# A row transform and an inverse product in the TensorE: the table becomes the stationary operand, the results are turned through device memory

## The chip, the cores and the metric

The kernel runs on one core of a Trainium2 chip. The metric is the device time of one launch, in microseconds (us); lower is better. Engines are called as the profile calls them: PE (matmuls) and PEld (PE's loads of its stationary operand), DVE, ACT, POOL, and SP, which here only issues DMAs.

## What is computed

64 images of 96 channels and 56 x 56 pixels go through three blocks. The reference, cut to what matters:

```python
# block 1: expand 96->192 (1x1) + silu, shift, 3x3 depthwise + identity + silu, gate, project 192->96, + x, silu
# block 2, per image, h of 192 channels over 3136 pixels in a row:
h = relu(bn(einsum('bnc,hc->bnh', layernorm(x), w1)))
X = jnp.fft.fft(h, axis=1, norm='ortho')          # along the 3136 pixels
xr = relu(X.real * rd - X.imag * idg + rb)        # and xi likewise
# ... inverse transform of the real result, product with w2 (192->96), bn, + x
# block 3: layernorm, 96->384->96 with 8-bit and 16-bit rounding, + x
```

The transform of length 3136 = 56 x 56 is done in two steps, each of them a product with a table of cosines and sines: first along one of the two factors ("rows", step f1), then along the other (step f2). Because the input is real, only 29 of the 56 frequencies of the first step are kept (NK = 29). On the way back, after the product with w2, step i1 multiplies by the table of the second factor and step i2 by that of the first.

## The kernel before

**Order of the work.** Every image is cut into named steps (ea_mm, dw_mm, ..., o_st), each a small function that issues one group of instructions; a name's ending tells the engine: `_mm` PE, `_ev` an evacuation by ACT (or DVE for w1_ev and i2_ev), `_ld`, `_st`, `_in` a DMA issued by SP. The table PLAN (L43) holds a time for every instance of every step and PERIOD (L42) the distance between images. The loop at L944 to L951 sorts all instances of all 64 images by `b * PERIOD + when` and issues them in that order. The times set nothing but this order: each engine works through its own instructions in it and waits by semaphores for what they need. So in the middle of the run PE works on parts of three or four images by turns, and an instruction that waits holds up all that PE has behind it.

**The steps around the change**, for one image:

- w1_mm (L642): 8 groups of matmuls, in each of them up to 8 columns of 56 pixels for both halves of the channels (hc), into one of two shared PSUM buffers of 2 banks (`mix_ps`, L378; w1, f1, f2, w2, i1 and i2 take them by turns). w1_ev (L658, DVE) applies relu and the scale and writes `buf_h`, channel by channel, 56 pixels each; partitions 0 to 55 hold channels 0 to 95, partitions 64 to 119 channels 96 to 191.
- f1_mm (L671): for each of 96 channel pairs the image's 56 columns are the stationary operand and the table `f_tab` streams (58 columns), twice, into both halves of PSUM's partitions: 192 products in 6 groups. f1_ev (L685, ACT): 12 copies into `buf_g`.
- f2_mm (L696): product with `l_tab`; f2_u, f2_s, f2_r, f2_p (ACT and DVE): the frequency filter, into `buf_h` (pq_a, pq_b). w2_mm (L762) and w2_ev (L790): product with w2, back into `buf_g` (u_v).
- i1_mm (L802): for each of 96 output channels a 112 x 32 block of `u_v` is the stationary operand and `inv_tab` streams (56 columns), for r = 0 and 1: 192 products in 3 groups of 64. i1_ev (L818, ACT): 3 copies into `buf_h` (p_v).
- i2_mm (L823): 112 products in 4 groups; a 64 x 48 block of p_v is stationary, 56 columns of `r_tab` stream; two of them lie in opposite quarters of the array. i2_ev (L840, DVE): 8 additions onto the image `t`.
- Then n_*, x_* (layer norm and turning), h_*, o_* (block 3), o_st (output by SP).

A product of 32-bit operands takes two passes, each a weight load (LDWEIGHTS) and a matmul of its own in the profile, so all these counts double there: 384 pairs per image at L676 (f1), 384 at L809 (i1), 224 at L831 (i2).

**DMAs.** In the loop SP issues, per image, 14 loads of x (L192), 14 stores of the output (L932) and 2 small transfers (L635). In the setup POOL issues ten loads between memsets (L216 to L347), ACT some others.

## Time and profile before

| what | value |
|---|---|
| median of 3 runs | 7425.91 us (7415.92 to 7431.19) |
| profiled execution: span from first to last instruction | 7414.7 us, 11.2 us under the median |
| PE / PEld / DVE / ACT / POOL busy | 7188.3 / 5229.7 / 4842.3 / 4641.4 / 1589.9 us |
| PE instructions | 177666 matmuls and as many weight loads |
| granted TensorE clock, mean | 0.993 |
| DMA | 185.34 MB, mean 25 GB/s |

The profile's page lists busy time by engine, the span in 40 slices, the DMA queues, the chain of work that ended last, and the costliest groups of instructions by line; "issue" means that an engine stood still and waited for nothing that the profile shows. The times in the text that go beyond the page come from the groups by line and shape, the order in time, and the waits of the same trace.

### The profile page before, as it was taken

Reading aid. Unit: us, or ns where it says so; the run is one execution under the profiler, and the core shown is the slowest. Engines: PE = TensorE matmul, PEld = TensorE weight load, DVE = VectorE, ACT = ScalarE, POOL = GpSimd, SP = SyncE. Lnnn points to the kernel's source line nnn. Section 1 sums busy time; section 2 is a strip of 40 time slices with the busy share of each in tenths; the row PEclk is TensorE's granted clock in tenths of the full one; section 3 lists DMA queues with packets and bytes.
Section 4 is the critical chain, followed back from the end, with each engine's and each line's share of the span. In section 5 each row is a group of like instructions: output and inputs, shape, how many; then the busy total and the mean of one; then the engine's idle time right before and its main releaser. Section 6 shows DMA issues by size and latency. Waiting matters only on the chain.

```text
span 7414.7 us, 383547 instructions
## 1 busy us (share of the span) xinstructions
PE 7188.3 (97%) x177666; PEld 5229.7 (71%) x177666; DVE 4842.3 (65%) x8790; ACT 4641.4 (63%) x9806; POOL 1589.9 (21%) x1366
## 2 busy tenths in 40 slices
PE   7999999999999999999999999999999999999997
PEld 5777777777777777777777777777777777777775
DVE  5666667666666666666666666666666666666674
ACT  3566666566665666666656666566666666666665
POOL 1221222212212122122121221221212212212222
PEclk9999999999999999999999999999999999999998
DMA  2010110110101101011011011110110111101100
GB/s 52 18 28 20 28 27 19 28 24 23 28 20 28 26 20 28 21 27 28 18 29 26 20 28 23 25 27 19 30 26 20 28 23 24 28 20 28 27 20 21
DMA packets 424334, 185.34 MB, mean 25 GB/s; under 512 B 378786, under 2 KB 422042, under 8 KB 422474
## 3 DMA queue, kind: packets, MB, share of 16 engines
q1 hardware_dynamic: 420794, 159.01, 9.3%
q8 instruction: 1392, 22.81, 1.3%
q0 software_dynamic: 528, 1.50, 0.1%
q14 instruction: 212, 1.73, 0.1%
q10 hardware_dynamic: 1408, 0.28, 0.0%
HBM read 82.80 MB, written 77.07 MB: 22 GB/s over the span
## 4 chain that ended last, share of the span: by engine, by line
PE 93%; ACT 3%; issue 3%; DVE 1%; POOL 0%; DMA 0%; POOLq 0%; ACTq 0%; SPq 0%
PE ps_d L469 14%; PE psa L676 9%; PE psa L649 9%; PE ps_ea L406 5%; PE ps_eb L423 5%; PE psa L831 5%; PE ps_n L580 5%; PE ps_pj L555 5%; PE psa L768 5%; PE psa L809 4%; PE ps_c L580 4%; PE psa L703 4%; PE ps_h L888 4%; PE ps_o L910 3%; PE psa L713 3%
## 5 line engine op out<-in xcount | busy, mean ns | idle before, releaser
L926 POOL TENSOR_TENSOR o<-t,o 112x448 f32<-112x448 f32 x448 | 659.1, 1471 | 3629.9 <-DVE o L920 2280.0
L469 PE MATMUL ps_d<-e_a,diag 32*32 32x392 f32 x36864 | 1029.5, 498 | 0.7 <-ACT d L479 0.7
L898 DVE TENSOR_SCALAR y<-y,qb 128x448 f16<-128x448 f16 x1344 | 483.1, 384 | 761.5 <-ACT y L893 748.4
L491 DVE SCALAR_TENSOR_TENSOR d_last<-e_b,taps,d_last 128x1568 f32<-128x1568 f32 x512 | 972.5, 1899 | 9.3
L469 PEld LDWEIGHTS ps_d<-e_a,diag 32*32 32x32 f32 x36864 | 659.8, 103 | 299.6 <-issue 37.5
L591 DVE TENSOR_REDUCE v<-sq 112x4 f32<-112x384 f32 x896 | 490.6, 548 | 480.7 <-ACT sq L587 479.7
L893 ACT CAST y<-ps_h 128x448 f16<-128x448 f32 x1344 | 682.6, 543 | 165.7 <-PE ps_h L888 157.8
L860 POOL TENSOR_TENSOR rs<-v,mhalf 112x4 f32<-112x4 f32 x448 | 489.5, 1097 | 1264.2 <-DVE v L592 1264.2
L649 PEld LDWEIGHTS psa<-w1c,t 112*64 112x64 f32 x14336 | 609.0, 137 | 178.0 <-issue 86.4
L904 ACT CAST h<-y 128x448 fp8e5<-128x448 f16 x1344 | 733.0, 570 | 2.2 <-DVE y L898 2.0
L676 PEld LDWEIGHTS psa<-f_tab,buf_h 128*56 128x56 f32 x24576 | 650.4, 131 | 111.0 <-ACT buf_g L688 45.4
L649 PE MATMUL psa<-w1c,t 112*64 112x96 f32 x14336 | 688.4, 249 | 3.4 <-DVE buf_h L661 1.8
L676 PE MATMUL psa<-f_tab,buf_h 128*56 128x58 f32 x24576 | 675.6, 216 | 1.1 <-DVE buf_h L661 1.1
L609 POOL TENSOR_TENSOR rs<-v,mhalf 112x4 f32<-112x4 f32 x448 | 461.1, 1034 | 917.2 <-DVE v L592 763.3
L566 DVE TENSOR_TENSOR ps_pj<-ps_pj,x 112x392 f32<-112x392 f32 x512 | 260.6, 566 | 546.0 <-issue 326.1
L572 ACT ACTIVATE t<-ps_pj,pjbn_b 112x392 f32<-112x392 f32 x512 | 289.6, 621 | 413.5 <-DVE ps_pj L566 413.5
L661 DVE SCALAR_TENSOR_TENSOR buf_h<-psa,rs_full 128x768 f32<-128x768 f32 (+1 forms) x512 | 430.8, 852 | 148.7 <-PE psa L649 148.7
L688 ACT COPY buf_g<-psa 128x464 f32<-128x464 f32 x768 | 388.8, 551 | 186.4 <-PE psa L676 184.7
L411 ACT ACTIVATE e_a<-ps_ea 128x448 f32<-128x448 f32 x448 | 237.6, 551 | 427.3 <-PE ps_ea L406 427.2
L809 PE MATMUL psa<-inv_tab,buf_g 112*32 112x56 f32 x24576 | 373.3, 214 | 99.3 <-issue 97.5
L809 PEld LDWEIGHTS psa<-inv_tab,buf_g 112*32 112x32 f32 x24576 | 327.5, 110 | 197.5 <-issue 196.3
L866 DVE TENSOR_TENSOR xt<-ps_n,rs 112x384 fp8e5<-112x384 f32 x448 | 243.7, 556 | 315.8 <-POOL rs L860 311.4
(176 smaller groups left out, 12984.4 us busy)
## 6 DMA issues: line engine op xcount, KB each, us to landing
x<-in_x SPq DMA_DIRECT2D x896, 84.0 KB, 2.7
out_dram<-o SPq DMA_DIRECT2D x896, 84.0 KB, 2.1
l_tab<-in_tab_l SPq DMA_DIRECT2D x1, 1624.0 KB, 6.9
r_tab<-in_tab_r SPq DMA_DIRECT2D x1, 1568.0 KB
t<-dev_t SPq DMA_DIRECT2D x64, 7.0 KB, 1.8
t<-dev_t SPq DMA_DIRECT2D x64, 5.2 KB
ex_row_p<-in_expand_row POOLq DMA_DIRECT2D x1, 336.0 KB, 4.3
s_p<-in_bn POOLq DMA_DIRECT2D x1, 288.0 KB, 4.6
```

What stands on the lines that cost most here:

```text
L469: nc.tensor.matmul(pss[r][j * 32 : j * 32 + 32], lhsT=diag[pr, tap, :], rhs=e_a[pr, r0 : r0 + PJ, dx : dx + HW], start=tap == 0, stop=tap ...
L491: nc.vector.scalar_tensor_tensor(d_last, win, w, d_last, ALU.mult, ALU.add)
L580: nc.tensor.matmul(cen[c0:c1, k, 0:C], lhsT=t_of(b)[:, n0 + c0 : n0 + c1], rhs=center, start=True, stop=True)
L591: nc.vector.tensor_reduce(v, sq, AX.X, ALU.add)
L649: nc.tensor.matmul(ps[hc * 64 : hc * 64 + 64, k, 0:C], lhsT=t[:, n0 : n0 + 64], rhs=w1c[:, hc * C : hc * C + C], start=True, stop=True,)
L676: nc.tensor.matmul(ps[r * 64 : r * 64 + HW, k, 0 : 2 * NK], lhsT=buf_h[:, n0 : n0 + HW], rhs=f_tab[:, r, :], start=True, stop=True,)
L809: nc.tensor.matmul(ps[p0 : p0 + 32, k, 0:HW], lhsT=u_v[:, oh * 48 + o, :], rhs=inv_tab[:, r, :], start=True, stop=True,)
L860: nc.gpsimd.tensor_tensor(rs, held.pop(("nv", b, g)), mhalf[0:CP, 0:4], ALU.pow)
L893: nc.scalar.copy(y16, held.pop(("h", b, i)))
L898: nc.vector.tensor_scalar(y16, y16, qb1[:, i % 3 : i % 3 + 1], 0.0, ALU.add, ALU.max)
L904: nc.scalar.copy(held["h8", b, j][:, m, :], held.pop(("y", b, i)), saturate=False)
L926: nc.gpsimd.tensor_tensor(o32, rows, o16, ALU.add)
```

## The change

Four things are done together.

- **f1.** The table is the stationary operand (`f_tab`, now 56 rows by 64 columns, for both halves of the partitions), and the image streams: 4 columns of pixels by 96 channels, 384 columns in one product. There are 7 groups of 4 products, one for each half of the channels (hc, the upper or lower half of the array's rows) and each parity of the pixel column (d, the left or right half of its columns). So w1_ev now writes `buf_h` pixel by pixel. The result has the frequency on the partitions, where f2 wants the pixel column there; f1_ev (7 copies) puts it into a work tile `fs`, f1_st (new, SP) stores it to device memory (`spec`), and f2_ld (new, SP, 12 per image) loads it turned into `buf_g`.
- **i1.** `inv_tab` (112 x 112) is stationary and `u_v` streams in pieces of 5 x 96 = 480 columns (the last of 384): 6 products in 3 groups. i1_ev (6 copies) writes `q_v` in `buf_g`, i1_st (new, 3 per image) stores it to device memory (`rows`), i2_ld (new, 8 per image) loads it turned into p_v. w2_ev writes u_v in the order in which it streams.
- **i2.** p_v has the 112 output rows (96 and a gap) side by side and half as many pixel columns, the two parities of the pixel column lying on the two halves of the partitions: 56 products in 4 groups of 14; a 64 x 112 block is stationary, 56 columns of `r_tab` stream. `r_tab` is half as long.
- **The table of times** is new throughout, with PERIOD = 103.2569549 in place of 116.1319138; and the ten setup loads of POOL go to ACT's queue, with a smaller scratch area for POOL's DMAs.

The diff, without most of the table's rows, without the rest of the setup's loads, which change `nc.gpsimd` to `nc.scalar` in the same way, and without the reordering of `r_tab`:

```diff
-PERIOD = 116.1319138
+PERIOD = 103.2569549
 PLAN = {
...
+    "f1_mm": (75.0170900, 75.8761200, 80.2152800, 81.5140300, 91.9872400, 92.1258300, 99.3428400),
+    "f1_st": (78.0873900, 81.9866100, 83.7293200, 86.5475800, 92.3438400, 99.8859600, 101.3793700),
+    "f2_ld": (
+        102.4924500, 106.8217200, 102.5435000, 110.1029100, 102.0934200, 105.7929300, 101.6237600, 104.9552400,
+        103.3621800, 120.0976500, 102.9367900, 115.2317000,
+    ),
+    "f2_mm": (114.8964200, 112.8360300, 119.7091400, 122.9963600, 126.2902700, 131.1408300),
+    "i1_mm": (143.7804000, 150.4246800, 153.4075700),
+    "i1_st": (152.7400300, 153.9883000, 154.5288200),
+    "i2_ld": (161.7438100, 158.8409100, 159.6870200, 158.6831700, 171.8823200, 165.2089400, 170.9082900, 168.8317300),
+    "i2_mm": (168.4278800, 169.6223400, 173.7120700, 171.8985100),
...
+    dram = ctx.enter_context(tc.tile_pool(name="dram", bufs=2, space=bass.MemoryType.DRAM))
...
-        nc.gpsimd.dma_start(out=b[0:rows], in_=src.rearrange("(o f) c -> o f c", o=1).to_broadcast([rows, 4, n]))
+        nc.scalar.dma_start(out=b[0:rows], in_=src.rearrange("(o f) c -> o f c", o=1).to_broadcast([rows, 4, n]))
...
-    f_tab = load(tab_f, [128, 2, 2 * NK], "f_tab", nc.scalar)
+    f_tab = load(tab_f, [128, 64], "f_tab", nc.scalar)
...
-    r_tab = load(tab_r, [128, HW, HW], "r_tab")
+    r_tab = load(tab_r, [128, NJ, HW], "r_tab")
-    h_v = buf_h[:, 0 : C * HW].rearrange("p (c b) -> p c b", b=HW)
+    h_v = buf_h[:, 0 : C * HW].rearrange("p (b c) -> p b c", c=C)
     pq_a = buf_h[:, 0 : NK * CP].rearrange("p (k f) -> p k f", f=CP)
     pq_b = buf_h[:, NK * CP : (NK + NS) * CP].rearrange("p (k f) -> p k f", f=CP)
-    p_v = buf_h[:, 0 : 48 * HW].rearrange("p (b o) -> p b o", o=48)
-
-    buf_g = const.tile([128, NK * MID], F32, name="buf_g")
+    p_v = buf_h[:, 0 : NJ * CP].rearrange("p (b o) -> p b o", o=CP)
+
+    buf_g = const.tile([128, NK * C + 32 * 128], F32, name="buf_g")
-    g_v = buf_g.rearrange("p (k c) -> p k c", c=MID)
-    u_v = buf_g[0:CP, 0 : C * 32].rearrange("p (o k) -> p o k", k=32)
+    g_v = buf_g[:, 0 : NK * MID].rearrange("p (k c) -> p k c", c=MID)
+    u_v = buf_g[0:CP, 0 : NK * C]
+    q_v = buf_g[0:CP, NK * C :].rearrange("p (k o) -> p k o", o=128)
         d, j0, n = W1[g]
         ps = held.pop(("w1", b, g))
         nc.vector.scalar_tensor_tensor(
-            h_v[:, :, d * NJ + j0 : d * NJ + j0 + n],
-            ps[:, 0:n, 0:C].rearrange("p b c -> p c b"),
+            h_v[:, d * NJ + j0 : d * NJ + j0 + n, :],
+            ps[:, 0:n, 0:C],
             0.0,
-            rs_full[:, d, j0 : j0 + n].unsqueeze(1).to_broadcast([128, C, n]),
+            rs_full[:, d, j0 : j0 + n].unsqueeze(2).to_broadcast([128, n, C]),
             ALU.max,
             ALU.mult,
         )
     def f1_mm(b, g):
-        ps = mix_ps(c=16, k=64)
-        for k in range(16):
-            n0 = (g * 16 + k) * HW
-            for r in range(2):
+        ps = mix_ps(h=2, n=512)
+        for hc in range(2):
+            for d in range(2):
+                n0 = d * NJ + g * 4
                 nc.tensor.matmul(
-                    ps[r * 64 : r * 64 + HW, k, 0 : 2 * NK],
-                    lhsT=buf_h[:, n0 : n0 + HW],
-                    rhs=f_tab[:, r, :],
+                    ps[d * 64 : d * 64 + 64, hc, 0 : 4 * C],
+                    lhsT=f_tab[hc * 64 : hc * 64 + HW, :],
+                    rhs=h_v[hc * 64 : hc * 64 + HW, n0 : n0 + 4, :],
                     start=True,
                     stop=True,
                 )
         held["f1", b, g] = ps
-    def f1_ev(b, n):
-        g, hc = divmod(n, 2)
-        c0 = hc * C + g * 16
-        nc.scalar.copy(
-            g_v[:, :, c0 : c0 + 16],
-            held["f1", b, g][:, :, hc * NK : hc * NK + NK].rearrange("p c k -> p k c"),
+    def f1_ev(b, g):
+        fs = work.tile([128, 4, 2, C], F32, tag="fs", name="fs")
+        ps = held.pop(("f1", b, g))
+        nc.scalar.copy(fs.rearrange("p b h c -> p h b c"), ps[:, :, 0 : 4 * C].rearrange("p h (b c) -> p h b c", c=C))
+        held["fs", b, g] = fs
+
+    def f1_st(b, g):
+        if ("spec", b) not in held:
+            held["spec", b] = dram.tile([128, NJ, MID], F32, tag="spec", name="spec")
+        fs = held.pop(("fs", b, g))
+        nc.sync.dma_start(
+            out=held["spec", b][:, g * 4 : g * 4 + 4, :], in_=fs.rearrange("p b h c -> p b (h c)")
+        )
+
+    LD = ((0, 8), (8, 16), (16, NK))
+
+    def f2_ld(b, m):
+        i, p = divmod(m, 4)
+        r, d = divmod(p, 2)
+        k0, k1 = LD[i]
+        p0, q0 = r * 64 + d * NJ, d * 64 + r * 32
+        nc.sync.dma_start(
+            out=g_v[p0 : p0 + NJ, k0:k1, :], in_=held["spec", b][q0 + k0 : q0 + k1].rearrange("k b c -> b k c")
         )
         for src, n in parts:
-            nc.scalar.copy(u_v[:, :, at : at + n], src.rearrange("p k o -> p o k"))
+            nc.scalar.copy(u_v[:, at * C : (at + n) * C].rearrange("p (k o) -> p k o", o=C), src)
     def i1_mm(b, g):
-        ps = mix_ps(o=16, b=64)
-        for k in range(16):
-            o = g * 16 + k
-            for oh in range(2):
-                for r in range(2):
-                    p0 = oh * 64 + r * 32
-                    nc.tensor.matmul(
-                        ps[p0 : p0 + 32, k, 0:HW],
-                        lhsT=u_v[:, oh * 48 + o, :],
-                        rhs=inv_tab[:, r, :],
-                        start=True,
-                        stop=True,
-                    )
+        ps = mix_ps(u=2, n=512)
+        for u in range(2):
+            c0 = (g * 2 + u) * 5 * C
+            c1 = min(c0 + 5 * C, NK * C)
+            nc.tensor.matmul(
+                ps[0:CP, u, 0 : c1 - c0],
+                lhsT=inv_tab.rearrange("p r n -> p (r n)"),
+                rhs=u_v[:, c0:c1],
+                start=True,
+                stop=True,
+            )
         held["i1", b, g] = ps
-    def i1_ev(b, g):
-        ps = held.pop(("i1", b, g))
-        nc.scalar.copy(p_v[:, :, g * 16 : g * 16 + 16], ps[:, :, 0:HW].rearrange("p o b -> p b o"))
+    def i1_ev(b, n):
+        g, u = divmod(n, 2)
+        k0, k1 = n * 5, min(n * 5 + 5, NK)
+        nc.scalar.copy(
+            q_v[:, k0:k1, :].rearrange("p k (e o) -> p k e o", e=2)[:, :, :, 0:48],
+            held["i1", b, g][0:CP, u, 0 : (k1 - k0) * C].rearrange("p (k e o) -> p k e o", e=2, o=48),
+        )
+
+    def i1_st(b, g):
+        if ("rows", b) not in held:
+            held["rows", b] = dram.tile([CP, 32, CP], F32, tag="rows", name="rows")
+        ks = slice(g * 10, g * 10 + 10 if g < 2 else 32)
+        nc.sync.dma_start(out=held["rows", b][:, ks, :], in_=q_v[:, ks, 0:CP])
+
+    def i2_ld(b, m):
+        h, p = divmod(m, 4)
+        d, r = divmod(p, 2)
+        p0 = d * 64 + r * 32
+        src = held["rows", b][r * HW : r * HW + HW].rearrange("(n d) k o -> d k n o", d=2)
+        ns = slice(h * 14, h * 14 + 14)
+        nc.sync.dma_start(out=p_v[p0 : p0 + 32, ns, :], in_=src[d, :, ns, :])
     def i2_mm(b, g):
         ps = mix_ps(u=2, k=8, a=64)
-        for turn in range(2):
-            for k in range(7):
-                for bk in range(2):
-                    oh = turn ^ bk
-                    n2 = g * 14 + bk * 7 + k
-                    pr = slice(oh * 64, oh * 64 + 64)
-                    nc.tensor.matmul(
-                        ps[oh * 64 : oh * 64 + 48, bk, k, 0:HW],
-                        lhsT=buf_h[pr, n2 * 48 : n2 * 48 + 48],
-                        rhs=r_tab[pr, n2, :],
-                        start=True,
-                        stop=True,
-                    )
+        for k in range(7):
+            for d in range(2):
+                pr = slice(d * 64, d * 64 + 64)
+                nc.tensor.matmul(
+                    ps[0:CP, d, k, 0:HW],
+                    lhsT=p_v[pr, g * 7 + k, :],
+                    rhs=r_tab[pr, g * 7 + k, :],
+                    start=True,
+                    stop=True,
+                )
         held["i2", b, g] = ps
     def i2_ev(b, n):
-        g, bk = divmod(n, 2)
-        n0 = (g * 14 + bk * 7) * HW
-        cols = t_of(b)[:, n0 : n0 + 7 * HW].rearrange("p (k a) -> p k a", a=HW)
-        nc.vector.scalar_tensor_tensor(cols, held["i2", b, g][0:CP, bk, 0:7, 0:HW], b2_sh, cols, ALU.add, ALU.add)
+        g, d = divmod(n, 2)
+        cols = t_of(b)[:, 0:NPIX].rearrange("p (n d a) -> p n d a", d=2, a=HW)[:, g * 7 : g * 7 + 7, d, :]
+        nc.vector.scalar_tensor_tensor(cols, held["i2", b, g][0:CP, d, 0:7, 0:HW], b2_sh, cols, ALU.add, ALU.add)
...
-    f = np.zeros((128, 2, 2 * NK))
+    f = np.zeros((128, 64))
     for h in range(2):
-        f[64 * h : 64 * h + HW, 0, h * NK : (h + 1) * NK] = np.cos(a) / HW
-        f[64 * h : 64 * h + HW, 1, h * NK : (h + 1) * NK] = -np.sin(a) / HW
+        f[64 * h : 64 * h + HW, 0:NK] = np.cos(a) / HW
+        f[64 * h : 64 * h + HW, 32 : 32 + NK] = -np.sin(a) / HW
     t["f"] = f
...
-    nc = bacc.Bacc("TRN2", target_bir_lowering=False, num_devices=1)
+    nc = bacc.Bacc("TRN2", target_bir_lowering=False, num_devices=1, dynamic_dma_scratch_size=2048)
```

## Prediction

> **What bounds the kernel now.** I read the busy time by engine first, then the slices, then the waits of PE, then the order in time.
>
> ```profile
> PE 7188.3 (97%) x177666; PEld 5229.7 (71%) x177666; DVE 4842.3 (65%) x8790; ACT 4641.4 (63%) x9806; POOL 1589.9 (21%) x1366
> PE   7999999999999999999999999999999999999997
> ...
> L676 PE MATMUL psa<-f_tab,buf_h 128*56 128x58 f32 x24576 | 675.6, 216 | 1.1 <-DVE buf_h L661 1.1
> L809 PE MATMUL psa<-inv_tab,buf_g 112*32 112x56 f32 x24576 | 373.3, 214 | 99.3 <-issue 97.5
> ```
>
> PE is full in all slices but the first and the last, and the chain that ended last is 93% PE. Its waits, longest first:
>
> ```profile
> PE psa L809 <- issue: 97.5, 112, 2.0
> PE ps_w1c L324 <- DVE w1s L322: 26.2, 1, 26.2
> PE ps_c L580 <- issue: 24.5, 23, 2.9
> PE ps_se L501 <- ACT d L479: 16.4, 65, 1.3
> ```
>
> So once the setup is over PE waits for hardly anything but "issue", that is, for nothing that the profile shows. So what counts is PE's time per image. I add up, in the middle of the run, from each matmul's start to the next one's: 114.1 us per image, 64 of them 7303 us, the other 112 us being start, filling and draining. Of the 114.1, f1 (L676) has 10.36, i1 (L809) 7.17, i2 (L831) 5.78, c_mm (L580) 5.51.
>
> **What a matmul costs here.** These lines are from the order in time of one image:
>
> ```profile
> 3471.30 0.88 PE L780 MATMUL psa<-w2b,buf_h 64*64 64x96 f32 x32
> 3472.16 1.03 PE L768 MATMUL psa<-w2a,buf_h 128*64 128x96 f32 x20
> ```
> ```profile
> 3486.54 1.57 PE L560 MATMUL ps_pj<-d_last,pw 64*112 64x392 f32 x8
> 3488.05 1.78 PE L809 MATMUL psa<-inv_tab,buf_g 112*32 112x56 f32 x128
> ...
> 3493.97 1.37 PE L809 MATMUL psa<-inv_tab,buf_g 112*32 112x56 f32 x90
> 3496.49 0.69 PE L809 MATMUL psa<-inv_tab,buf_g 112*32 112x56 f32 x38 [1.15 <-issue]
> ```
>
> L780 runs four 64x64 tiles at a time: 32 matmuls are 8 rounds of 96 columns, 768 columns one after the other, in 0.86 us (3471.30 to 3472.16). L560 runs the two halves of the rows at a time: 4 rounds of 392 columns, 1568, in 1.51 us. So a column costs about 0.83 ns and a group some 0.2 us to get going. The old groups fit: f1's is 32 rounds of 58, 1856 columns, 1.74 us by this rule and 10.36 / 6 = 1.73 in the trace. The last line shows the stall in i1: after 90 of 128 matmuls PE stands for 1.15 us.
>
> **The change, part by part, per image.**
>
> *f1.* Out: 10.36 us. In: 7 groups of 4 products, each a quarter of the array as in L780, so 2 passes of 384 columns, 768 in all: 0.84 us, seven times 5.9. Difference -4.5.
>
> *i1.* Out: 7.17 us, 1.71 of it in stalls of over 0.6 us between two matmuls. In: 12 passes over the whole array, 1920 columns in each of two groups and 1728 in the third: 1.79 + 1.79 + 1.63 = 5.2. Difference -2.0. The stalls come where 128 short pairs of loads and matmuls follow each other in 1.7 us; PE's 5552 instructions per image become 3928 (812 pairs of load and matmul fewer: 328 in f1, 372 in i1, 112 in i2), so I also let the gaps at c_mm go that follow i1: -0.4. If they stay, 27 us are lost.
>
> *i2.* Here the halving of the matmuls brings nothing, because the weight load grows from 48 to 112 columns while only 56 stream. Out: 5.78. The nearest row is L626, 128 columns loaded for 16 that stream:
>
> ```profile
> 3509.27 0.62 PE L626 MATMUL ps_rs<-rs,sel 112*128 112x16 f32 x4
> 3509.82 0.87 PE L580 MATMUL ps_n<-center,t 112*64 112x96 f32 x16
> ```
>
> Four in 0.55 us, 0.14 each; the weight loads inside start 0.11 us apart (3509.27, 3509.38, 3509.49). So 112 columns take 0.096 us, against 0.05 for the streaming. L560 has the new shape of load (64x112) on both halves of the rows and keeps its rounds at streaming speed, so the two halves load side by side. In: 4 groups of 14 rounds of 0.096 and 0.2 to start: 6.2. Difference +0.4. Bounds: 3.5 if the load were hidden behind the streaming (-2.3), 11.6 if the two halves load one after the other (+5.8). I take the middle, as it is L626's own spacing.
>
> [...]
>
> *ACT and DVE.* f1_ev: 7 copies of 768 elements at 807 ns (L798's row of that size) for 12 at 551: 5.6 for 6.1 us (388.8 / 64). i1_ev: 6 of about 0.55 for 3 of 0.92: +0.5. DVE's counts stay; w1_ev now writes in a row, at most 0.1 us less each. They hold 72 and 76 us per image, under a PE at 108: nothing.
>
> *The turns through device memory.* These are the new waits. SP gets 30 more DMAs per image beside its 30, at 0.62 us each in its densest burst:
>
> ```profile
> 3490.22 6.19 SPq L192 DMA_DIRECT2D x<-in_x  x10
> ```
>
> 30 times 0.62 is 19 us of 108; SP has room. But SP works in order: f2_ld waits for the last f1_st to have landed, and loads and stores of x and the output behind it wait with it. They are issued early enough by the table (x_in stands at least 10 us ahead of its ea_mm) to bear some 5 us.
>
> PE is in order as well, and all three images in work stand behind a late f2_mm. So the turn must fit into the PE work which the new table puts between. Read off by sorting the table: between f1_mm's last group (99.34) and the first f2_mm (112.84) stand four ea_mm, three dw_mm, two h_mm, one o_mm: 4 x 0.89 + 3 x 2.65 + 2 x 0.24 + 0.68 = 12.7 us. The turn: f1_ev 0.8; f1_st 2.1 (the output's landing of 84 KB) and 0.8 for 300 KB more (the l_tab's 1624 KB landed in 6.9 us, x's 84 in 2.7: 2.7 ns per KB); ten loads, the last issued after 9 x 0.62 = 5.6 and landed 2.9 later. Sum 12.2: covered, with 0.5 to spare. Between the last i1_mm and the first i2_mm stand 12.3 us (seven c_mm, three ea_mm, seven h_mm, three o_mm, one sp_mm); the turn: copies 1.4, i1_st 588 KB 3.5, four loads 1.9 + 3.0: 9.8, with 2.5 to spare. I charge 0.3 us per image for the first turn, and bound it from 0 to 3 us.
>
> [...]
>
> *Start and end.* The setup's loads move from POOL, where memsets stand between them, to ACT; PE's first matmul waits 26.2 us for their chain. ACT's own DMA issues take 0.33 to 0.59 us. Gain or loss of some us, taken as 0. When the last image is alone, the turns lie open, some 22 us for two, less what image 62 still has to do: +20.
>
> **Sum** on the profiled execution: per image -4.5 - 2.0 - 0.4 + 0.4 + 0.3 = -6.2, times 64 = -397; 7414.7 - 397 + 20 = 7038; the median lies 11.2 above the span: **7050 us**, 5% less than 7425.9.
>
> **Rivals.**
>
> (a) i2's loads hide behind the streaming: 2.7 us per image less, 7050 - 173 = 6877. For: L831 streams at full speed with 48-column loads. Against: L626. Chance 0.08.
>
> (b) i2's two halves load one after the other: +5.4 x 64, 7396, a small gain only. Against: L560's rounds, 1.51 us for four, which two loads one after the other would also fit under 392 columns, so L560 doesn't exclude it fully. Chance 0.06.
>
> (c) The change doesn't overlap what it says: f1's quarters run only two at a time, 0.64 us more per group, +287: 7337. Against: L780. Chance 0.03.
>
> (d) The first turn overruns its cover by 1 to 5 us, at f2_mm: 7110 + up to 256. For: 0.5 us to spare is less than the error of its terms. Chance 0.13 for more than 7160.
>
> (e) Slower: the same turn, at the first f2_mm. It decides from (7426 - 7050) / 64 = 5.9 us per image beyond what I charge, that is when f1_st's landing and the ten loads take 18 us and not 11.4. At 25 us PE would stand 13 us per image: 7870. Against: x and the output land in 2.7 and 2.1 us in this very trace, and the DMA engines are busy under a tenth of the time. Chance 0.06.
>
> **How the numbers follow.** The forecast, 6940 to 7160, has 0.64. The range of 8 in 10 takes in (a) and the nearer half of (d): 6870 to 7240. Under 0.2% (15 us) can't be told from no change by such measurements. Faster: 0.64 + 0.08 + 0.03 + 0.12 + half of (b) = 0.90; the other half of (b) and the ends of (d) are the same, 0.04; slower 0.06.
>
> **What would show it.** Right: f1's group at about 0.84 us from its first matmul to the next line's, i1's at 1.8 without an idle "issue" inside, i2's 28 matmuls at 1.5 us with weight loads 0.1 us apart; PE busy still above 95% of the middle slices. Wrong: waits of f2_mm or i2_mm on a DMA in the tens of us in total or more (d, e); i2 groups of 0.9 us (a) or 2.9 us (b); DVE or ACT above 80% with PE waiting for them.

## The result and the profile after

The changed kernel takes 8110.6 us against 7428.2 (medians of four runs each), ratio 1.0911 (95% interval 1.089 to 1.0932): 9% slower where 5% faster was forecast. One run of it, of 8417 us at a lower clock, is left out of the ratio. The profiled execution has 8106.6 us of span; its mean granted clock is 0.903, before 0.993.

From the page after: the busy line, the granted clock by slice, the DMA queue that SP fills and the one that brings PE's instructions.

```profile
PE 7422.9 (92%) x125698; PEld 5048.5 (62%) x125698; DVE 4772.5 (59%) x8790; ACT 4629.5 (57%) x9678; POOL 1584.9 (20%) x1355
...
PEclk9899889898998899999989989989889999998897
...
q1 hardware_dynamic: 1173946, 699.66, 37.2%
q8 instruction: 989, 16.20, 0.9%
```

PE has 51968 matmuls fewer and yet 235 us more of busy time, and its idle time has grown from 226 to 684 us. In 15 of the 40 slices the granted clock is under 0.9, before in one. The trace's records of the clock hold 1 or a half and nothing between (178 of each after, 16 of each before), so the mean gives the time at half clock: 8106.6 x 0.097 x 2 = 1573 us, before 7414.7 x 0.007 x 2 = 104. A stretch at a half is called a drop below.

The groups by line and shape show that the new products are what they were meant to be, except one:

```profile
L677 PE MATMUL psa<-buf_h,f_tab 56*64 56x384 f32 x3584 | 350.8, 497 | 1.5 <-DVE buf_h L662 1.4
L825 PE MATMUL psa<-buf_g,inv_tab 112*112 112x480 f32 x640 | 290.2, 584 | 0.0
L862 PE MATMUL psa<-r_tab,buf_h 64*112 64x56 f32 x7168 | 627.4, 356 | 120.8 <-DMA buf_h<-rows 117.9
```

From each matmul's start to the next one's, per image in the middle of the run: f1 (L677) 5.16 us, i1 (L825) 4.95 without a pause inside, c_mm 4.91 where it was 5.51; but i2 (L862) 9.71 where it was 5.78, and dw_mm 22.42 where it was 15.90. A wait behind a matmul counts with it here. The period has gone from 114.1 to 124.3 us.

The waits of PE, where "issue" headed the list with 97.5 us at i1:

```profile
PE ps_d L470 <- issue: 193.2, 64, 5.6
PE psa L862 <- DMA buf_h<-rows: 117.9, 67, 6.2
PE ps_se L517 <- ACT red L509: 89.1, 64, 2.2
PE psa L731 <- DMA buf_g<-spec: 58.9, 16, 15.0
```

Both turns show (L862, L731), but the longest wait has no releaser and stands in dw_mm, which the change doesn't touch. The order in time of one image, PE:

```profile
3937.36 5.47 PE L862 MATMUL psa<-r_tab,buf_h 64*112 64x56 f32 x56 [1.38 <-DMA buf_h<-rows]
...
3986.21 7.78 PE L470 MATMUL ps_d<-e_a,diag 32*32 32x392 f32 x257
3997.38 0.95 PE L470 MATMUL ps_d<-e_a,diag 32*32 32x392 f32 x31 [3.39 <-issue]
```

and the same image in stretches (length, busy time of PE, PEld, DVE, ACT, POOL, then granted clock, DMA share, GB/s):

```profile
3923.00:3937.30 14.30, 12.06 (x158) 7.37 (x156) 7.54 (x23) 12.70 (x31) 9.49 (x9) 1.00 0.92 193
3937.30:3950.00 12.70, 12.64 (x118) 11.37 (x118) 3.60 (x8) 0.97 (x2) 0.00 (x0) 0.51 0.38 57
3950.00:3955.00 5.00, 5.00 (x57) 4.66 (x56) 1.83 (x4) 0.91 (x3) 0.78 (x1) 0.53 0.20 39
3955.00:3986.00 31.00, 31.00 (x500) 19.52 (x495) 20.64 (x39) 21.64 (x45) 8.79 (x9) 1.00 0.31 108
3986.00:3999.00 13.00, 8.94 (x292) 5.00 (x288) 12.90 (x11) 1.90 (x5) 2.79 (x1) 1.00 0.93 186
3999.00:4003.00 4.00, 3.94 (x41) 3.42 (x43) 0.00 (x0) 2.11 (x9) 0.00 (x0) 0.57 0.15 29
```

Three things stand here. In the second and third row, after a wait of 1.4 us for the rows, the clock is at a half for 17 us; each half of i2 takes 5.5 us, where the forecast's 1.5 us a group make 3, and n_mm and w1_mm behind it are slow too (2.50 us for 32 products at L650, where 32 take 1.49 at clock 1.00). In the fifth row the twelve loads of the spectrum hold the DMA engines at 93% for 13 us; PE runs dw_mm for 8 us on the instructions it has and then stands, and the DMA records show why: one packet of 16 KB of instructions at 3985.8, the next only at 3994.6, where dw_mm uses one in some 3.5 us (1152 instructions per image in the 15.90 us of before). It is the same in the other images: the 989 packets, at 256 instructions each, are 253184, where the trace has 253201 of PE, and in the count of PE's instructions the 46 pauses of over 1 us in dw_mm all begin a multiple of 256 apart. PE goes on 1.5 us, with a spread of 0.1, after a packet has landed. In the sixth row, after that pause, the clock has dropped again.

### The profile page after: what moved, and what is told of

It is laid out like the page before. It is cut to its first block, busy times and chain, and to the rows that moved or that the text cites. A ratio compares the mean times of both kernels' runs of the same rounds, so it can differ in the third digit from the quotient of the medians.

```text
span 8106.6 us, 283340 instructions
## 1 busy us (share of the span) xinstructions
PE 7422.9 (92%) x125698; PEld 5048.5 (62%) x125698; DVE 4772.5 (59%) x8790; ACT 4629.5 (57%) x9678; POOL 1584.9 (20%) x1355
## 3 DMA queue, kind: packets, MB, share of 16 engines
q8 instruction: 989, 16.20, 0.9%
q14 instruction: 236, 1.93, 0.1%
## 4 chain that ended last, share of the span: by engine, by line
PE 71%; DMA 8%; DVE 8%; ACT 6%; issue 5%; SPq 2%; POOL 0%; ACTq 0%; POOLq 0%; DVEq 0%
PE ps_d L470 9%; PE psa L650 8%; PE psa L862 8%; PE psa L786 5%; PE ps_eb L424 5%; PE ps_n L581 4%; PE ps_pj L556 4%; PE psa L677 4%; DMA buf_h<-rows 4%; PE psa L825 4%; DVE s L762 3%; DVE ue L765 3%; PE ps_c L581 3%; PE psa L721 3%; DMA buf_g<-spec 2%
## 5 line engine op out<-in xcount | busy, mean ns | idle before, releaser
L470 PE MATMUL ps_d<-e_a,diag 32*32 32x392 f32 x36864 | 1160.5, 517 | 194.5 <-issue 193.2
L650 PE MATMUL psa<-w1c,t 112*64 112x96 f32 x14336 | 744.1, 264 | 0.5 <-ACT fs L689 0.5
L862 PE MATMUL psa<-r_tab,buf_h 64*112 64x56 f32 x7168 | 627.4, 356 | 120.8 <-DMA buf_h<-rows 117.9
L862 PEld LDWEIGHTS psa<-r_tab,buf_h 64*112 64x112 f32 x7168 | 607.6, 268 | 182.2 <-issue 131.6
L480 ACT ACTIVATE d<-ps_d,mid_b 128x392 f32<-128x392 f32 x512 | 293.0, 583 | 749.3 <-PE ps_d L470 749.3
L874 DVE SCALAR_TENSOR_TENSOR t<-psa,bn2c_b,t 112x392 f32<-112x392 f32 x512 | 296.8, 621 | 715.4 <-PE psa L862 715.4
L650 PEld LDWEIGHTS psa<-w1c,t 112*64 112x64 f32 x14336 | 688.6, 150 | 34.1 <-issue 23.3
L588 ACT ACTIVATE sq<-ps_n 112x384 f32<-112x384 f32 x448 | 214.0, 492 | 564.7 <-PE ps_n L581 563.9
L775 DVE SCALAR_TENSOR_TENSOR buf_h<-ue,s 128x448 f32<-128x448 f32 (+2 forms) x768 | 407.5, 579 | 131.9 <-ACT s L769 131.9
L945 ACT CAST o<-ps_o 112x448 f16<-112x448 f32 x448 | 236.9, 548 | 414.1 <-PE ps_o L940 406.1
L407 PE MATMUL ps_ea<-x,ex_w 112*32 112x448 f32 x3584 | 444.5, 549 | 17.6 <-DMA x<-in_x 16.5
```

The source lines that it names most:

```text
L407: nc.tensor.matmul(ps[qs], lhsT=ex_w[:, qs], rhs=window(q, j * RPC, RPC), start=True, stop=True)
L470: nc.tensor.matmul(pss[r][j * 32 : j * 32 + 32], lhsT=diag[pr, tap, :], rhs=e_a[pr, r0 : r0 + PJ, dx : dx + HW], start=tap == 0, stop=tap ...
L650: nc.tensor.matmul(ps[hc * 64 : hc * 64 + 64, k, 0:C], lhsT=t[:, n0 : n0 + 64], rhs=w1c[:, hc * C : hc * C + C], start=True, stop=True,)
L862: nc.tensor.matmul(ps[0:CP, d, k, 0:HW], lhsT=p_v[pr, g * 7 + k, :], rhs=r_tab[pr, g * 7 + k, :], start=True, stop=True,)
```

## The experiments

Theory T: the excess over the forecast is made by PE's pauses, each paid twice, once itself and once in the clock that it drops; the pauses come from the two turns, the first because one burst of loads holds up PE's instruction fetch and f2_mm, the second because the loads of the rows are late. Rival R1: i2's products, whose weight loads are longer than their streaming (0.096 us against 0.05 by the prediction's estimate), drop the clock by themselves. Rival R2: dw_mm's stall has nothing to do with the burst. Later rivals are in the expectations. Times of single runs stand beside 7419 to 7443 us of the kernel before on the same chip; the half-clock time is worked out as above. The diffs are shortened: several lines are drawn together, `...` stands for what is left out, and notes behind `#` are added.

### e1 to e4: the quarters, and the loads left out

```diff
 # e1
+                for c0, c1 in TILES:
                     nc.tensor.matmul(
-                    ps[0:CP, d, k, 0:HW], lhsT=p_v[pr, g * 7 + k, :],
+                        ps[c0:c1, d, k, 0:HW], lhsT=p_v[pr, g * 7 + k, c0:c1],
 # e2 (e4: both)
+        if b == 0:
             nc.sync.dma_start(out=p_v[p0 : p0 + 32, ns, :], in_=src[d, :, ns, :])
 # e3 (e4: both)
+        if b == 0:
             nc.sync.dma_start(out=g_v[p0 : p0 + NJ, k0:k1, :], in_=...)
-                        lhsT=g_v[:, k1, c0 : c0 + 64],
+                        lhsT=l_tab[:, k1, c0 * 3 // 4 : c0 * 3 // 4 + 64],
```

> Each product of the second inverse is cut in two by its stationary columns (64 and 48), so that four quarters of the array work at once as in the kernel before; the loads and waits stay. T (the pause ahead of the second inverse, and the other pauses, drop the granted clock): the drop still begins at the wait for the rows, the four groups of 28 become 56 products each and take about 1.5 us a group at half clock where 2.7 now, and the time is about 7810 us. R1 (halves of the array that wait for their weight loads are themselves what drops the clock): the drop of 46 images at this line goes, a group takes about 0.9 us, and the time is about 7520 us.

> The eight loads of the rows are issued for the first image alone; in every other image the second inverse takes what the step before left in that buffer (so it leaves out the second turn through device memory, not its stores). T: without the wait the clock no longer drops there, a group of the second inverse takes about 1.5 us instead of 2.7, the mean clock is 0.95 or more, and the time is about 7570 us. R1: the groups stay near 2.7 us at half clock and only the wait goes, about 7990 us.

> The twelve loads of the spectrum are issued for the first image alone, and the column products take a constant table as their stationary operand (so it leaves out the first turn's loads, not its stores). T: the idle time of the depthwise products put down to issue (193 us) falls below 30, the wait of the column products (59 us) goes, and the time is about 7690 us. R2 (the issue stall has another cause than the burst of loads): the depthwise issue time stays near 190 us, and the time is about 7960 us.

> Both of the last two: no loads of the spectrum and none of the rows after the first image. T: the mean clock is 0.98 or more and the time 7050 to 7150 us, near what was forecast. R1: the second inverse is still at half clock, about 7480 us.

| run | us | clock | half-clock us | PE's waits at i2 / dw "issue" / spectrum | i2 per image |
|---|---|---|---|---|---|
| after | 8110.6 | 0.903 | 1573 | 118 / 193 / 59 | 9.71 |
| e1 | 7716.0 | 0.950 | 771 | 161 / 185 / 61 | 4.9 |
| e2 | 7540.5 | 0.959 | 618 | 4 / 212 / 41 | 5.78 |
| e3 | 7749.5 | 0.919 | 1255 | 123 / 4 / 0 | 10.2 |
| e4 | 7144.5 | 0.979 | 300 | 4 / 4 / 0 | 5.78 |

e2, e3 and e4 lie within 1% of what T gave, e1 lies between T and R1. R1 as it stands falls with e2. Same products, no wait, and the clock records show one drop that begins at i2 where there were 46. Its groups by line, and the two halves of one image's i2 in time:

```profile
L863 PE MATMUL psa<-r_tab,buf_h 64*112 64x56 f32 x7168 | 388.3, 263 | 3.9 <-DMA buf_h<-rows 3.9
```
```profile
3904.53 2.96 PE L863 MATMUL psa<-r_tab,buf_h 64*112 64x56 f32 x56
3908.32 2.96 PE L863 MATMUL psa<-r_tab,buf_h 64*112 64x56 f32 x56
```

But e1 shows that the form of the products matters as well: with the wait still there (161 us) the clock drops at i2 in 31 images, and yet 392 us are gone:

```profile
4009.91 3.33 PE L863 MATMUL psa<-r_tab,buf_h 64*64 64x56 f32 x112 [1.52 <-DMA buf_h<-rows]
4014.87 1.93 PE L863 MATMUL psa<-r_tab,buf_h 64*64 64x56 f32 x112 [0.74 <-DMA buf_h<-rows]
```

The first half is slow (3.33 us), the second already at full clock (1.93). So a pause starts the drop here, and the clock stays down longer with products of 64 rows by 112 columns behind it than with the same work in quarters: 8.1 us at half clock per image at i2 after, 2.2 in e1. Whether that is for the time in which their weight loads hold up the streaming or for another difference of the two forms, no run separates. The drops in "after" are multiples of 3.41 us long, 113 of the 178 one or two of these, and all 59 that follow a pause ahead of i2 four to six.

Not every pause does it. Take PE's pauses of over 0.7 us, and count a drop as a pause's own when it begins between the pause's start and 3.41 us after its end; 177 of the 178 drops in "after" have such a pause. There 59 of 65 pauses ahead of i2 (1.8 us on average) are followed by a drop, of 16.3 us on average; 45 of 52 in dw_mm (3.6 us), of 5.3; 46 of 63 at the gate (L517, 1.4 us), of 3.8. But in e4 only 1 of 60 pauses of 1.2 us at f2 is, beside 53 of 63 at the gate, and in the kernel before 4 of 69 pauses of 1.2 us at i1. The waits of e4:

```profile
PE ps_se L517 <- ACT red L509: 88.9, 64, 2.2
PE psa L732 <- DVE ue L766: 73.2, 63, 2.4
```

So the half clock behind a pause differed here with its length and with what follows it, and the pauses of 1.2 us at f2 and i1, 5 of 129 with a drop, cost hardly more than themselves. How much of it is for the length and how much for what follows, these places don't separate.

R2 falls with e3: without the burst dw_mm's issue wait is 4 us.

```profile
PE ps_d L470 <- issue: 4.1, 1, 4.1
```

And e4, with neither, is 94 us above the forecast: the two turns are nearly all of the miss. The double payment can be counted in sum: from after to e2 118 - 4 us of waits go and 955 us of half clock, worth half of that: 114 + 477 = 591 against 568 measured; from after to e4 193 + 118 + 59 and 33 of "issue" at f2, less 8 that stay and 34 more for DVE at f2 and w2, are 361; 361 + 636 = 997 against 964.

### e5 to e11: moving loads and steps

```diff
 # e5: four pieces by pixel column, each loaded behind its two stores
-    LD = ((0, 8), (8, 16), (16, NK))
+    LD = ((0, 8), (8, 16), (16, 24), (24, NJ))
-            out=g_v[p0 : p0 + NJ, k0:k1, :], in_=held["spec", b][q0 + k0 : q0 + k1].rearrange("k b c -> b k c")
+            out=g_v[p0 + j0 : p0 + j1, :, :], in_=held["spec", b, i][q0 : q0 + NK].rearrange("k b c -> b k c")
 # e6: x_in 1 to 3, o_st 1
-    "x_in": (-63.1929400, -53.2542300, -51.4288100, -48.0565100, ...
+    "x_in": (-63.1929, -62.8139, -62.6139, -62.4139, ...
-    "o_st": (249.4914500, 258.4491800, ...
+    "o_st": (249.4914, 275.7570, ...
 # e9
-    "i2_ld": (161.74, 158.84, 159.69, 158.68, 171.88, 165.21, 170.91, 168.83),
+    "i2_ld": (154.66, 154.62, 154.64, 154.60, 155.15, 155.12, 155.14, 155.13),
 # e10 (and lt, ls 7 us later)
-    "eb_mm": (-14.03, -10.68, -14.16, -9.41, -12.37),
+    "eb_mm": (-2.36, -2.16, -2.41, -2.10, -2.26),
```

> The spectrum goes to device memory in four pieces by pixel columns, and each piece is loaded as soon as its two stores have landed, during the row transform, so that only a seventh of the data is left for the last burst; bytes are the same, loads are 16 instead of 12. T (one burst of 13 us that fills the DMA engines holds up the instruction fetch and the column products): the issue time of the depthwise products falls from 193 us to below 40, the waits for the spectrum go, about 7750 us, as without the loads. Rival S (the bytes themselves hold up the fetch, wherever they run): the same issue time of 150 us or more turns up in the row products and the row transform, and the time stays above 7950 us.

> Only the table is changed: three input loads are issued some 10 us earlier and one store of the output 17 us later, so that nothing stands ahead of the loads of the rows in SP's queue. T (the second turn is late for its place in SP's queue): the wait for the rows falls from 118 us to below 40, the drops of the clock that begin at the second inverse go from 46 to fewer than 20, about 7650 us. Rival Q (the turn is longer than its cover anyway): the wait shrinks by less than half, the clock still drops there, 7950 to 8100 us.

> The kernel before, its own row transform and inverses, with the times of the new table for all steps that both have (its six row transforms stand after the last row products, its first inverse after the last product of the second mixing). T: the order by itself costs little, 7400 to 7550 us, clock 0.98 or more. Rival U (the new order of the other steps is what costs the time, by new waits): 7700 us or more, with the depthwise issue time at 100 us or more.

> Table only: the eight loads of the rows are put right behind the stores of the first inverse in SP's queue, ahead of three steps that stood there (one third input load stays between the two halves of the loads); nothing else moves. T (the second turn is late for its place in the queue): the wait for the rows falls from 118 us to below 50, fewer than 25 drops of the clock begin at the second inverse where 46 did, 7650 to 7850 us. Rival Q (the turn is longer than its cover wherever the loads stand): the wait shrinks by less than half, the drops stay above 35, 7950 us or more.

> Table only: the five expansions of the last quarter (5.7 us of the array) are moved from between the row products into the first turn, ahead of the other expansions, and the nine steps on VectorE that wait for them 7 us later; the loads of the spectrum stay one burst. T (the burst holds up the instruction fetch of the depthwise products, which need 16 KB each 3.5 us, and the waits of the column products): the burst now lies beside long products that need few instructions, so the depthwise issue time falls from 193 us to below 80 and the wait for the spectrum goes, 7780 to 7900 us. Rival S (the fetch is held up whatever runs beside the burst): the issue time turns up at the expansions instead, 8000 us or more.

> The two edits of the table together with the second inverse in four quarters. T: the gains add, mean clock 0.97 or more, 7150 to 7350 us, faster than the kernel before. Rivals Q and S: one of the two waits and its half clock stay, 7450 us or more.

In all six the time is far over what T gave, and over the kernel before: 9780, 8154, 8016, 8680, 8526 and 8512 us.

- e5: a piece of 8 or 4 partitions is loaded slowly (41 to 87 GB/s in three stretches of such loads, where the twelve loads of the change had 186; more under e18), SP stands behind it, the next store waits in SP's queue, ScalarE for its work tile (909 us at f1_ev), and PE for ScalarE (825 us at o_mm). Its 753 us of waits for the spectrum come on top.
- e6 sums the wrong image: three loads of x now come before pj_add has read the image before. Its waits speak for Q all the same. Nothing stands ahead of the loads of the rows any more, but they stand still until i1_st has landed, some 5 us behind the stores' issue (326 us in all); the wait for the rows is 114 us, and 56 drops begin at i2. SP and PE in time:

```profile
3938.80 3.82 SPq L846 DMA_DIRECT2D rows<-buf_g  x3
3947.75 3.66 SPq L854 DMA_DIRECT2D buf_h<-rows  x7
```
```profile
3953.93 3.97 PE L862 MATMUL psa<-r_tab,buf_h 64*112 64x56 f32 x56 [1.22 <-DMA buf_h<-rows]
```

  From the end of the last i1_mm (3941.3) to the first i2_mm the turn takes 12.6 us, where it took 14.5 in the changed kernel, and PE has 11.4 us of work for it.
- e8 overwrites one of the first inverse's three groups before its copy (the work is the same). 433 us of half clock only, but new waits: 310 us at the first inverse, 89 at se, 141 at f2 and w2 for DVE. The table by itself, without the products that it was made for, costs 8%; how much of that is a bad fit of its f1 and i1 is open.
- e9 removes the wait at i2 (9 us) and shows that a pause at another line ahead of i2 does the same: the loads of x now land late,

```profile
3928.81 1.71 PE L407 MATMUL ps_ea<-x,ex_w 112*32 112x448 f32 x4 [5.06 <-DMA x<-in_x]
```

  546 us in all at ea_mm; in 62 images a drop begins there, of 25 us on average, and i2 behind it stays at 9.8 us. The loads of the rows had stood still in SP's queue for 5.1 us each image (334 us), until i1_st had landed, with x_in behind them.
- e10 put expansions where T wanted few instructions. But the burst begins some 4 us after the last f1_mm and goes on for 13, so that the expansions, old and moved, are over in the middle of it; dw_mm stalls as before (237 us), and f2 now waits 243 us for DVE. e11 has the waits of e9 and e10 together.

A run (e7) with the edits of e5, e6 and e1 together, for which T gave 7130 to 7230 us, took 9439 and shows what e5 shows.

### e12 to e18: the burst itself

```diff
 # e12
-  held["spec", b] = dram.tile([128, NJ, MID], ...)     # load: rows of 768 bytes
+  held["spec", b] = dram.tile([NJ, 128, MID], ...)     # load: 6 or 10 KB a partition
 # e13: rows the same, table inv[:, :, b], and
-    "o_st": (..., 258.4491800, ...)
+    "o_st": (..., 263.7570, ...)
 # e15: dram.tile([2, NJ, 64, MID]) and [2, 32, HW, CP]; one load fills 56 or 64 partitions
 # e16
+    def f2_go(b, i):
+        nc.scalar.copy(go, g_v[:, LD[2][0], 0:1])     # at 111.76, behind dw_ev 0; last four f2_ld at 112.1 to 112.4
 # e18 on e17
-            out=p_v[p0 : p0 + 32, ns, :], in_=held["rows", b][:, q0 : q0 + 14, :]
+            out=p_v[p0 : p0 + NK, ns, :], in_=held["rows", b][0:NK, q0 : q0 + 14, :]
-    "se2_mm": (29.1657100,),
+    "se2_mm": (30.0930,),
```

> The spectrum lies in device memory with the pixel column outermost, so that each of the twelve loads reads one contiguous stretch a partition (6 or 10 KB) instead of rows of 768 bytes; the seven stores write the rows of 768 bytes instead, spread over the row transform. Bytes, loads, order and table are unchanged. T (the length of the burst, which is that of its many small packets, holds up the instruction fetch): the burst falls from 13 us to about 7, the depthwise issue time from 193 us to below 70, the wait for the spectrum to near 0, 7700 to 7850 us. Rival V (the fetch is held up by the number of outstanding loads or by the bytes, not by the small packets): the burst or the issue time stays above two thirds of what it was, 7950 us or more.

> The same for the second turn: the rows lie in device memory with the frequency outermost and the pixel columns in the order of the loads (the inverse's table is permuted for it), so that each load reads contiguous stretches of 6 KB, and one store of the output that stood ahead of the loads in SP's queue goes behind them. The first turn is unchanged. T (a pause of a microsecond or two ahead of the second inverse drops the clock for all of it): the wait for the rows falls from 118 us to below 30, the drops that begin at the second inverse from 46 to below 15, a group takes near 1.5 us, 7550 to 7750 us. Rival Q: the wait stays above half of what it was, 7950 us or more.

> Both of the last two and the second inverse in four quarters. T: 7100 to 7250 us, mean clock 0.97 or more, faster than the kernel before (ratio 0.955 to 0.975). Rivals V and Q: above 7428 us, no gain on the kernel before.

> The contiguous layouts and the quarters of the run before, with the layouts turned once more so that one load writes 56 or 64 partitions where it wrote 28 or 32: six loads of the spectrum instead of twelve, four of the rows instead of eight, and stores in two halves. Bytes are the same. T with theory P (the load's rate goes with the partitions that one load writes: 28 partitions gave about 190 GB/s, 8 gave 54): the spectrum's burst falls from 13 us to 7 or 8, the depthwise issue time from 184 us to below 80, and the time is 7150 to 7350 us, faster than the kernel before. Rival B (the bytes themselves take 13 us on the way into the chip's memory, however they are split): the burst stays at 12 us or more, 7430 to 7520 us, no gain on the 7502 us of the run before but for shorter queues.

> The change with the twelve loads of the spectrum in two bursts: the first eight as they are, the last four (frequencies that the fourth column product is the first to need) held back until a one-element copy on ScalarE has run behind the first eviction of the depthwise products. Bytes, layouts and the rest of the table are unchanged; sixty-four such copies are added. T (an unbroken burst of 13 us starves the instruction fetch of the depthwise products, which run about 8 us on what is already fetched): two bursts of about 7 and 6 us with a gap leave time to fetch, the depthwise issue time falls from 193 us to below 80 and the waits for the spectrum go, 7750 to 7900 us. Rival S (the bytes hold up the fetch wherever they run): the issue time moves to the column products and the second half of the depthwise products and stays above 150 us together, 8000 us or more.

> The paced loads, the contiguous layouts of both turns with the output store behind the loads of the rows, and the second inverse in four quarters. T: 7200 to 7400 us, mean clock 0.97 or more, faster than the kernel before and than the 7502 us without the pacing. Rival S: 7480 us or more.

> The paced version with two edits more: the second turn stores and loads the 29 frequencies that are used instead of 32 (9% fewer bytes), and the second product of the gate stands 0.6 us later on TensorE, behind two feed-forward products, where it waited 1.4 us for ScalarE. T (every pause of a microsecond is paid once itself and once more in the clock): the wait of the gate falls from 89 us to below 60, that for the rows from 95 us to below 70, 7330 to 7420 us, faster than the kernel before by 0.2 to 1.3%. Rival: the pauses only move, 7430 to 7460 us, no difference from the kernel before.

| run | us | ratio to before | dw "issue" | wait for rows | half-clock us |
|---|---|---|---|---|---|
| e12 | 8075.6 | | 182 | 120 | 1502 |
| e13 | 7968.6 | | 193 | 91 | 1402 |
| e14 | 7501.6 | 1.0096 (1.0079 to 1.0113) | 184 | 90 | 555 |
| e15 | 7675.5 | 1.0328 (1.0311 to 1.0345) | 244 | 134 | 704 |
| e16 | 8067.0 | | 200 | 121 | 1532 |
| e17 | 7446.9 | 1.0018 (1.0008 to 1.0028) | 191 | 95 | 566 |
| e18 | 10629.7 | 1.4306 (1.4286 to 1.4327) | 181 | 3060 | 3884 |

e13 speaks for Q: the wait for the rows shrinks by a quarter only, and 43 drops still begin at i2. Four loads of x still stand ahead of its loads of the rows, but in e6 none did, and the wait was there. So the second turn is too long for its cover and not only badly placed. What e14 gains on e13 are mostly the quarters (by themselves they gained 392 us in e1, e12's edit 33). Neither the packets (e12) nor the width of a load (e15) make the first turn's burst long: it stays at 12 to 13 us. e15 is slower than either of its forecasts, with more "issue" in dw_mm and more waiting for the rows; why is open. e16 split the burst, and the stall split with it:

```profile
PE ps_d L468 <- issue: 200.2, 97, 4.6
```

97 pauses instead of 64, the sum as before. So Rival S is right against T: what holds up the fetch are the loads beside dw_mm, in one burst or in two, and not one burst's length. Only the wait for the spectrum went (59 to 9 us). With the quarters, pacing and both layouts, e17 is level with the kernel before: 0.18% above, which by the bound of the prediction is no difference. No version that does the whole work beat it.

e18 was to shave 9% off the second turn's bytes and made it the slowest of all. The stretches show why. e17, loads of the spectrum to 28 partitions, then of the rows to 32:

```profile
3926.00:3932.00 6.00, 5.11 (x177) 2.86 (x175) 5.96 (x6) 0.68 (x2) 2.19 (x1) 1.00 0.88 212
...
3993.50:3998.50 5.00, 2.60 (x23) 1.30 (x21) 1.63 (x7) 3.96 (x11) 3.38 (x4) 0.99 1.00 243
```

e18, loads of the rows to 29:

```profile
3980.00:4008.00 28.00, 3.50 (x28) 1.50 (x26) 2.58 (x10) 4.96 (x13) 4.37 (x5) 0.64 0.06 26
```

The loads to 29 partitions moved 26 GB/s, those to 28 and to 32 moved 212 and 243. A DMA share of 0.06 is what one engine of 16 makes when it is busy all the time, 0.88 fourteen, 1.00 all; that so many carried these loads is an estimate from the shares, and why 29 partitions are loaded so slowly, no run shows. In rows of 768 bytes the share says less, as packets overlap there: the loads to 8 partitions of e5 show 0.64 (68 GB/s), and the change's twelve loads, to 28, show 1.00 at their end (189 GB/s), with some 20 packets under way. The later se2_mm gained nothing: 86 us, now in front of h_mm.

## Why the prediction was wrong

Two steps failed. The sum took every duration from rows at clock 1.00 and had no term for the granted clock, which lost some 735 us; and both turns were taken as covered, at 12.2 and 9.8 us, where they took 17 and 14.5 and held up PE at dw_mm, f2_mm and i2_mm for 403 us.

- **What a matmul costs**: right. A column at 0.83 ns and 0.2 us a group gave f1 5.9 and i1 5.2 us; they take 5.16 and 4.95. The pauses in i1 and at c_mm went, as forecast.
- **i2**, "6.2, difference +0.4": the weight load sets the pace, as said (in e2 28 pairs of products in 2.96 us, 0.106 each, where the estimate was 0.096 for the load and 0.05 for the streaming), and at full clock (e2) it takes 5.78, so no difference at all. In the changed kernel it takes 9.71. By the prediction's own sign for (b), groups of 2.9 us, that rival would be read here (2.7); e2 shows that it is the clock. The step took a duration from rows at clock 1.00 and didn't ask what the granted clock would be.
- **The first turn**, "ten loads, the last issued after 9 x 0.62 = 5.6 and landed 2.9 later": mis-sized. It priced the loads by SP's issue and the landing of one. From 3985.2, when SP issues the first, to 3999 they take 13.8 us, not 8.5, because the engines are busy for 13 us, at 0.93 and 186 GB/s, with 2436 KB:

```profile
3985.23 7.22 SPq L707 DMA_DIRECT2D buf_g<-spec  x12
```

  That is 5.3 ns per KB; the text had 2.7, from the growth of a landing with its size. A row for it was in the trace of before and was used in the same sentence: l_tab's whole 1624 KB in 6.9 us make 10 us for 2436 KB.
- **The second turn**, "9.8, with 2.5 to spare": mis-sized as well. In the changed kernel x_in and o_st stand between i1_st and i2_ld in SP's queue:

```profile
3923.06 1.17 SPq L846 DMA_DIRECT2D rows<-buf_g  x2
3924.32 3.05 SPq L192 DMA_DIRECT2D x<-in_x  x2
3927.48 2.01 SPq L962 DMA_DIRECT2D out_dram<-o  x2
3929.53 1.12 SPq L192 DMA_DIRECT2D x<-in_x  x2
3930.78 3.58 SPq L854 DMA_DIRECT2D buf_h<-rows  x7
```

  The text said that SP works in order and looked only at what waits behind the loads, not at what stands ahead of them. Here the turn takes 14.5 us, from the last i1_mm's end at 3922.9 to the first i2_mm at 3937.4. What stands ahead is the smaller part of the error: in e6, with nothing there, it takes 12.6 us. There i1_st lands some 5 us behind its issue and not 3.5 (in e9 too), and the loads take 6.2 us to the first i2_mm (3947.75 to 3953.93) and not 4.9. Why is not shown; the three stores and the loads go together, and the text priced each by itself.
- **Instruction fetch**: not in the sum. The text asked what a late load does to f2_mm; PE stood before that, in dw_mm, 193 us in all.
- **The granted clock**: not in the sum, and the largest term: 1573 - 104 us more at half clock, some 735 us. New waits make 557: 193 in dw_mm, 118 at i2, 59 and 33 at f2, 73 more at se (the new table puts the two products of the gate 0.6 us apart) and 81 more for DVE at f2 and w2. The products are 1.5 us per image better than forecast, -97. Sum 1195 over the forecast where 1069 were measured (8106.6 us of span against 7038). Two things are counted twice in it: the 0.3 us per image that the forecast had charged for the first turn, 19 us, and half of the 91 us in which PE stood still at half clock, 45. Some 60 us stay open.

Of the rivals (e) had the sign, but not the mechanism: it put all of the loss into a wait at f2_mm and made it decide from an 18 us turn. The turn took 17 us, from the last f1_mm's end at 3982 to the last landing, and the wait at f2_mm is 0.9 us per image. The sign that (d) and (e) shared, waits of f2_mm or i2_mm on a DMA in the tens of us, did show: 59 and 118.

## What to carry to other kernels

Price a pause of PE at its length and, behind it, the time until the clock is back: here a pause of 1.4 us was followed by up to 17 us at half clock, longest where products of 64 x 112 follow (16.3 us on average), while of 129 pauses of 1.2 us 5 had a drop behind them; cut such products into four quarters where they stand behind a wait that can't be removed (392 us in e1). Price a burst of DMA by its bytes over the rate of a row of the same direction, not by its issue (13.8 us here against 8.5), a chain of store and load by the bytes that go together, and count PE's own instruction packets among those that wait in it (193 us in dw_mm, 4 without the loads in e3). Before the number of partitions of a load is changed, look for a row with the new number: 29 partitions in place of 32 cost some 3180 us here, e18 against e17.

## What the runs showed of the hardware that was not expected

- Behind pauses of 1.4 us at the gate the clock dropped to a half in 53 of 63 cases in e4; behind pauses of 1.2 us at f2 in 1 of 60. The drops of the changed kernel last multiples of 3.41 us (178, from 3.41 to 27.3). In the 14.3 us ahead of the drop at 3937.6 PE was busy for 12.06.
- With i2 in four quarters the drops behind its pauses last 4.6 us on average (e1), with products of 64 x 112 they last 16.3 (59 in the changed kernel, of 13.7 to 20.5).
- PE's instructions came by DMA in packets of 16 KB, 256 instructions each (989 packets, 16.20 MB); beside a burst at 0.93 of the engines one came 8.7 us after the last, and dw_mm lasted 7.8 us on what it had.
- Loads from device memory to 28 or 32 partitions ran at 186 GB/s in a burst of pieces of 768 bytes, and at 206 to 243 (e14, e17) in pieces of 6 or 10 KB.
- Loads to 29 partitions ran at 26 GB/s (e18), loads to 32 at 243 (e17).
